# Softplus terms added on GpSimd and the head norm's factor kept in PSUM, in a two-layer block on one core

## The chip, the cores and the metric

One core of one Trainium2 chip runs the whole program. A core has five engines that take their instructions in order, each from a queue of its own, and wait for one another by semaphores: TensorE (PE: matmuls and weight loads), VectorE (DVE), ScalarE (ACT), GpSimd (POOL) and SyncE (SP, which here only issues DMAs). Data lies in SBUF; matmuls write PSUM, which VectorE and ScalarE can also read and write. The metric is the time of one execution on the device in microseconds, the median of the runs.

## The reference

2048 tokens (2 sequences of 1024) of width 512 pass four blocks, each followed by a layer norm of input plus output: linear attention with decay, a gated FFN whose hidden state passes a Walsh-Hadamard transform, a selective scan, and a second gated FFN. Two places matter here. The attention's output is gated, normed per head of 32 columns, and scaled:

```python
o = o * jax.nn.sigmoid(gate)
og = o.reshape(b, n, num_heads, hd)
og = og * jax.lax.rsqrt(jnp.mean(og * og, axis=-1, keepdims=True) + EPS)
return og.reshape(b, n, d) * w
```

and the scan's step width is a softplus, which multiplies the input:

```python
delta = jax.nn.softplus(dt + b_dt[None, None, :])
dA = jnp.exp(delta_t[:, :, None] * A[None])
dBu = (delta_t * u_t)[:, :, None] * B_t[:, None, :]
h = dA * h + dBu
```

All arithmetic is fp32.

## The kernel before

The tokens are cut into five groups, in this order: group 0 (256 tokens of sequence 0), group 1 (512 of sequence 1), group 2 (512 of sequence 0), group 3 (512 of sequence 1), group 4 (the last 256 of sequence 0). For each there are phases: V and A (values, then attention), F (first FFN), the scan, and f (second FFN). The second FFN of group 1 is split into a1 and b1, which with the first FFNs F0 and f0 (second FFN of group 0) serve as fillers: TensorE takes their work while an attention or a scan has none for it. The order of the end is V4, A4, b1, F4, f2, f3, f4.

Every operation is an `Op` with an engine, an estimated time, the buffers that it reads, writes, allocates and frees, and a priority. The class `Order` goes through all of them when the program is built: of the operations that could begin it takes the one that its own clock puts first, and so fixes each engine's order of instructions. An engine's instructions stay in that order on the chip, whatever the real times are. A changed estimate, engine or release of a buffer can thus change the order of everything behind it.

Four PSUM banks of 128x512 carry the tag "mm" and serve all matmul groups; the other four are two tiles "da" of two banks each, in which the scan's decays stand. An "mm" bank goes back to the planner when the operation that names it under `free` has run.

**The head norm** (in `block`, inside `attention`). The gated output stands in `oT` (SBUF; the trace shows it as xT). ScalarE squares it into `sg` (line 921), TensorE sums the squares of each head with a block matrix into an "mm" bank (line 931), ScalarE makes the factor in two steps (lines 939 and 940, `rstd`), both written into `sg`, and VectorE multiplies `oT` by the norm's weight and the factor in place (line 946, `scaled`). A group of 512 tokens has four such blocks with one multiply of 512 columns; a group of 256 has two blocks with two multiplies of 256 columns. That makes 16 blocks and 20 multiplies. The products L996 that follow (the output projection) read all blocks of `oT`.

**The softplus** (`Scan.softplus`). For each of four slices of 128 channels of a group, ScalarE takes the sum with the bias out of PSUM into `r` (tile pt, line 1297), then the absolute value, its exponential and logarithm in `a` (tile th, lines 1304 to 1306), and relu in `r` (line 1307). VectorE adds the two (line 1316). A DMA of SP's queue writes the result, delta, to DRAM; GpSimd multiplies it into `u` (line 1324); a second DMA of SP writes that. The scan's loads bring both back in another layout. Five groups of four slices make 20 adds.

**The scan** (per group, 64 units for 512 tokens or 32 for 256). GpSimd multiplies (line 1384, dbu), ScalarE exponentiates the decays into PSUM (line 1404), VectorE scans (line 1432) and multiplies by C (line 1445), and GpSimd sums the results into y by adds (lines 1475 and 1481) and, for every other unit, by a DMA of its own queue that accumulates. `ffn` has the line 1076, in which VectorE multiplies the two halves of a hidden tile: TensorE's second product (line 1099) waits for it. The transposes of the scan's result are line 1510, the add of the residual line 1525.

The estimates for one operation of n columns are, in us, 0.145 + 1.05e-3 n on VectorE (`dve`) and 0.15 + 2.25e-3 n on GpSimd (`pool`).

Of the kernel before, what the change touches and what calls it, by code (L numbers as in the profile page):

```python
# [10 lines left out]
AF = mybir.ActivationFunctionType  # L11
ALU = mybir.AluOpType
# [52 lines left out]
EXP, LOG, TANH, SILU = ("exp", "log"), ("log",), ("exp", "silu"), ("silu",)  # L65
# [144 lines left out]
def two_layers(  # L210
# [5 lines left out]
    nc = tc.nc  # L216
# [43 lines left out]
    def chunks(gi):  # L260
        return GROUPS[gi][2]

    def tokens(gi):
        return chunks(gi) * P
# [12 lines left out]
    def mm_us(n, cols):  # L277
        return n * max(cols * 4 / 2400 + 0.006, 0.28 if cols <= P else 0)

    def pe(us, fn, **kw):  # L280
        return Op("PE", us, fn, **kw)

    def dve(cols, fn, **kw):
        return Op("DVE", 0.145 + cols * 1.05e-3, fn, **kw)

    def act(cols, fn, **kw):
        return Op("ACT", 0.18 + cols * 0.81e-3, fn, **kw)

    def pool(cols, fn, **kw):
        return Op("POOL", 0.15 + cols * 2.25e-3, fn, **kw)  # L290

    def dma(nbytes, dst, src, eng="SP", **kw):
        of = {"SP": nc.sync, "ACT": nc.scalar, "POOL": nc.gpsimd}[eng]
        more = {k: kw.pop(k) for k in ("accum_op", "allow_slow_non_contiguous") if k in kw}
        us = 0.9 if eng == "POOL" else 0.06
        return Op(eng, us, lambda: of.dma_start(dst(), src(), **more), dma=nbytes, **kw)  # L296
# [99 lines left out]
    eps4 = cp.tile([P, 1], F32, name="eps4")  # L396
# [93 lines left out]
    def log_tables():  # L490

        if order.table != "log":
            nc.scalar.preload_act_table_set("natural_log_exp_and_others")  # L493
# [126 lines left out]
    def attention(gi, nxt, prio):  # L620
# [3 lines left out]
        n, T = chunks(gi), tokens(gi)  # L624
        S = CG // n
# [3 lines left out]
        oT = Columns(gi)  # L629
# [9 lines left out]
        parts = [Buf() for _ in range(VB)]  # L639

        def blocks(vb):
            return range(vb * S, (vb + 1) * S)
# [73 lines left out]
        def block(vb):  # L716

            kd, qd, own, sg = Buf(), Buf(), Buf(), Buf()
            bank = Buf()
# [159 lines left out]
            def outputs():  # L879
# [23 lines left out]
                r=[own, qd] + v2 + scs + ([] if first else [came]), a=[("mm", bank3)],  # L903
                free=[own, qd] + scs + (v2 if vb == VB - 1 else [])
# [7 lines left out]
            def gated():  # L912
                yield dve(
                    512, lambda: nc.vector.scalar_tensor_tensor(
                        o(), sg.t, 1.0, bank3.t, ALU.add, ALU.mult
                    ),
                    r=[sg, bank3] + ([oT.whole] if vb else []), w=[parts[vb]],
                    a=[] if vb else [("xT", oT.whole)], free=[bank3],
                )
                yield act(  # L920
                    512, lambda: nc.scalar.activation(
                        sg.t, o(), AF.Square, scale=1.0 / math.sqrt(HD)
                    ),
                    r=[parts[vb], oT.whole], w=[sg],
                )
                spawn(norm())

            def norm():
                bank = Buf()
                yield pe(  # L930
                    mm_us(1, 512), lambda: nc.tensor.matmul(
                        bank.t, blk, sg.t, start=True, stop=True
                    ),
                    r=[sg, consts_b], a=[("mm", bank)],
                )

                def rstd():
                    log_tables()
                    nc.scalar.activation(sg.t, bank.t, AF.Ln, bias=eps4)  # L939
                    nc.scalar.activation(sg.t, sg.t, AF.Exp, scale=-0.5)  # L940

                yield Op("ACT", 1.3, rstd, r=[bank], w=[sg], free=[bank], table=LOG)

                def scaled():
                    for s, eb in enumerate(blocks(vb)):
                        nc.vector.scalar_tensor_tensor(
                            oT.t[:, eb, :], oT.t[:, eb, :], nw_s[:, eb : eb + 1],
                            sg.t[:, s * T : (s + 1) * T], ALU.mult, ALU.mult,
                        )

                yield Op(
                    "DVE", 0.2 * S + 0.55, scaled, r=[sg, oT.whole], w=[parts[vb]], free=[sg]
                )
                normed[vb].written = parts[vb].written

# [249 lines left out]
    class Scan:  # L1205
# [83 lines left out]
        def softplus(self, k, bank, u):  # L1289

            T = self.T
            r = Buf()

            a = Buf()

            def shifted():
                nc.scalar.activation(
                    r.t[:, :T], bank.t[:, :T], AF.Identity, bias=bd_s[:, k : k + 1]
                )

            def logs():
                v = a.t[:, :T]
                log_tables()
                nc.scalar.activation(v, r.t[:, :T], AF.Abs)
                nc.scalar.activation(v, v, AF.Exp, scale=-1.0)
                nc.scalar.activation(v, v, AF.Ln, bias=one)
                nc.scalar.activation(r.t[:, :T], r.t[:, :T], AF.Relu)

            late = 1 if self.gi > 1 else 0
            yield act(T, shifted, r=[bank, scan_b], a=[("pt", r)], free=[bank])  # L1310
            yield Op(
                "ACT", 4 * (0.25 + T * 0.82e-3), logs, w=[r], a=[("th", a)], table=LOG,
                prio=late,
            )
            yield dve(
                T, lambda: nc.vector.tensor_add(r.t[:, :T], a.t[:, :T], r.t[:, :T]),
                r=[a], w=[r], free=[a], prio=late,
            )
            yield dma(
                KB256 * T // G, lambda: self.dd[0, :, k, :], lambda: r.t[:, :T], r=[r],  # L1320
                w=[self.parts_b[0][k]],
            )
            yield pool(
                T, lambda: nc.gpsimd.tensor_mul(u.t[:, k, :], r.t[:, :T], u.t[:, k, :]),
                r=[r, u.whole], w=[u_b := Buf()], free=[r],
            )
            yield dma(
                KB256 * T // G, lambda: self.dd[1, :, k, :], lambda: u.t[:, k, :],
                r=[u_b, u.whole], w=[self.parts_b[1][k]],
                free=[u.whole],  # L1330
            )
# [320 lines left out]
```

## Time and profile before

| what | value |
|---|---|
| runs | 1833.96, 1833.40, 1831.62 us |
| median | 1833.4 us |
| the profiled execution | 1834.95 us |
| its span, first to last instruction | 1833.2 us |
| mean granted TensorE clock | 0.989 |
| instructions of the program | 21,253 |
| HBM read and written | 253.12 and 22.54 MB |

| edited or touched | instructions | mean ns |
|---|---|---|
| head norm, logarithm (L939, ScalarE) 128x512 | 16 | 687 |
| head norm, exponential (L940, ScalarE) 128x512 | 16 | 630 |
| head norm, multiply (L946, VectorE) 128x256 | 8 | 482 |
| softplus multiply (L1324, GpSimd) 128x256 | 8 | 762 |
| scan (L1432, VectorE) 128x512 | 384 | 1226 to 1286 |
| product with C (L1445, VectorE) 128x1024 | 256 | 1223 |
| product du by B (L1384, GpSimd) 128x1024 | 256 | 2538 |

A busy share counts the time in which an engine executes; TensorE's matmuls are pipelined, so its share says little of how well it is used, but its gaps are gaps. An fp32 matmul appears as two records. "Idle before" a group is time in which its engine had nothing to execute just ahead of it, with what ended it. The granted clock is the share of its full speed that TensorE had.

### The profile page before, as it was taken

What the parts mean: (1) busy time and instruction counts of PE and PEld (TensorE: products, weight loads), DVE (VectorE), ACT (ScalarE), POOL (GpSimd) and SP (SyncE); (2) the same over time, 40 slices, a digit from 0 to 9 for tenths busy, and PEclk for the clock granted to TensorE, in tenths of its full rate; (3) what the DMA queues carried; (4) which work ended last, traced back from release to release, by engine and by line L of the source; (5) the groups of instructions that cost most, each with busy time, mean ns of one, the idle gap of its engine ahead of it and who ended that gap; (6) DMA issues with size and microseconds to landing.
All of it is one profiled execution on the core that took longest, in us unless ns stands there. A gap on an engine that the chain in (4) does not pass through costs nothing.

```text
span 1833.2 us, 21253 instructions
## 1 busy us (share of the span) xinstructions
PE 1769.9 (97%) x7064; PEld 1000.4 (55%) x7064; DVE 1308.5 (71%) x1557; ACT 1153.7 (63%) x1825; POOL 1069.8 (58%) x558
## 2 busy tenths in 40 slices
PE   7999999998999999999999999999999899999998
PEld 3556764443566644445675444577765344544574
DVE  6433115997699899926998999359998998998211
ACT  3634136688866776767766667676766757765321
POOL 0000004887477899824878888238899787786000
PEclk9999999999999999999999999999999999999999
DMA  9523435666657887736688676478988675766252
GB/s 265 180 68 106 149 128 166 179 179 173 230 138 217 245 212 207 192 113 197 171 255 232 167 207 181 143 243 236 282 234 222 187 199 167 199 169 166 75 174 85
DMA packets 227708, 336.32 MB, mean 183 GB/s; under 512 B 21264, under 2 KB 131216, under 8 KB 227600
## 3 DMA queue, kind: packets, MB, share of 16 engines
q1 hardware_dynamic: 209024, 271.53, 46.6%
q0 software_dynamic: 16272, 59.25, 17.1%
q10 hardware_dynamic: 2304, 4.20, 0.6%
q8 instruction: 56, 0.92, 0.2%
q14 instruction: 52, 0.43, 0.1%
HBM read 253.12 MB, written 22.54 MB: 150 GB/s over the span
## 4 chain that ended last, share of the span: by engine, by line
PE 67%; DVE 13%; ACT 8%; DMA 5%; issue 3%; POOL 3%; SPq 0%; DVEq 0%; ACTq 0%; POOLq 0%
PE mm L1045 35%; PE mm L1099 17%; DVE da L1432 6%; PE mm L653 4%; DMA y<-dbu 4%; PE mm L996 2%; PE mm L602 2%; POOL dbu L1384 2%; DVE dbu L1445 2%; ACT da L1404 2%; PE mm L840 1%; ACT L496 1%; ACT L1404 1%; PE mm L522 1%; ACT L493 1%
## 5 line engine op out<-in xcount | busy, mean ns | idle before, releaser
L1384 POOL TENSOR_TENSOR dbu<-du,B 128x1024 f32<-128x1024 f32 x256 | 646.9, 2538 | 141.3 <-DMA y<-dbu 107.8
L1045 PE MATMUL mm<-xT,w 128*128 128x512 f32 (+1 forms) x1912 | 669.1, 509 | 3.5 <-DVE h L1076 1.6
L1045 PEld LDWEIGHTS mm<-xT,w 128*128 128x128 f32 x1912 | 362.8, 190 | 308.4 <-issue 269.1
L1404 ACT ACTIVATE da<-delta,a_s 128x512 f32<-128x512 f32 (+1 forms) x640 | 384.3, 605 | 152.1 <-DVE dbu L1445 122.8
L1432 DVE TENSOR_TENSOR_SCAN da<-da,hlast,dbu 128x512 f32<-128x512 f32 (+1 forms) x384 | 425.7, 1109 | 34.0 <-ACT da L1404 20.4
L1099 PE MATMUL mm<-w,h 128*128 128x512 f32 x768 | 344.8, 605 | 9.7 <-DVE h L1076 7.4
L1481 POOL TENSOR_TENSOR y<-y,dbu 128x1024 f32<-128x1024 f32 x123 | 319.3, 2596 | 54.0 <-DVE dbu L1445 49.0
L1445 DVE TENSOR_TENSOR dbu<-da,C 128x1024 f32<-128x1024 f32 x256 | 313.1, 1223 | 14.9 <-ACT hlast L1457 7.9
L1432 DVE TENSOR_TENSOR_SCAN da<-da,dbu 128x256 f32<-128x256 f32 (+1 forms) x256 | 245.9, 960 | 20.9 <-ACT da L1404 14.9
L1099 PEld LDWEIGHTS mm<-w,h 128*128 128x128 f32 x768 | 147.6, 194 | 189.6 <-issue 170.4
L1045 PE MATMUL mm<-xf,w 128*128 128x256 f32 x1024 | 229.9, 383 | 2.3 <-ACT sg L939 1.4
L1045 PEld LDWEIGHTS mm<-xf,w 128*128 128x128 f32 x1024 | 194.7, 192 | 35.0 <-issue 4.6
L496 ACT ACT_TABLE_LOAD x140 | 179.6, 1283 | 6.9 <-PE mm L653 3.4
L496 ACT ACTIVATE h<-mm 128x512 f32<-128x512 f32 x144 | 85.7, 597 | 124.8 <-PE mm L1045 69.1
L1076 DVE TENSOR_TENSOR h<-h,mm 128x512 f32<-128x512 f32 x96 | 65.2, 679 | 101.8 <-PE mm L1045 94.7
L1404 ACT ACT_TABLE_LOAD x106 | 136.0, 1283 | 1.8
L653 PE MATMUL mm<-xT,w 128*128 128x512 f32 (+1 forms) x320 | 117.3, 514 | 7.6 <-DVE xn L1525 1.8
L1457 ACT COPY hlast<-da 128x2 f32<-128x2 f32 (+1 forms) x160 | 25.3, 158 | 156.1 <-DVE dbu L1445 140.1
L296 POOL DMA_DIRECT2D y<-dbu x113 | 107.8, 954 | 13.1 <-DVE dbu L1445 5.4
L743 POOL TENSOR_TENSOR qd<-h,q_dec 128x512 f32<-128x512 f32 x14 | 18.1, 1293 | 164.7 <-ACT h L496 104.5
L1099 PE MATMUL mm<-w,hf 128*128 128x512 f32 x256 | 112.5, 592 | 0.0
L1118 DVE TENSOR_TENSOR xn<-mm,xn 128x512 f32<-128x512 f32 x60 | 40.9, 682 | 93.8 <-PE mm L1099 93.8
(95 smaller groups left out, 1339.3 us busy)
## 6 DMA issues: line engine op xcount, KB each, us to landing
y<-dbu POOLq DMA_DIRECT2D x113, 512.0 KB, 6.1
w<-in_wgut_dram SPq DMA_DIRECT2D x192, 256.0 KB, 4.7
B<-rows SPq DMA_DIRECT2D x128, 256.0 KB, 4.7
C<-rows SPq DMA_DIRECT2D x128, 256.0 KB, 4.0
w<-in_wdnt_dram SPq DMA_DIRECT2D x96, 256.0 KB, 4.8
w<-in_w1t_dram SPq DMA_DIRECT2D x80, 256.0 KB, 4.4
w<-in_w3t_dram SPq DMA_DIRECT2D x80, 256.0 KB, 5.0
w<-w2h SPq DMA_DIRECT2D x80, 256.0 KB, 4.5
```

Source lines behind the costliest of these rows:

```text
L296: return Op(eng, us, lambda: of.dma_start(dst(), src(), **more), dma=nbytes, **kw)
L496: nc.scalar.activation(dst, src, AF.Silu)
L653: nc.tensor.matmul(bank.t[:, s * T : (s + 1) * T], w_qk[j][k].t[:, eb * P : (eb + 1) * P], xT.t[:, k, :], start=k == 0, stop=k == EB - 1,)
L1045: nc.tensor.matmul(bank.t[:, s * T + c0 * P : s * T + c1 * P], blocks[fb // 2][j][k // 2].t[:, k % 2 * 2 * P + k0 : k % 2 * 2 * P + k0 + P ...
L1076: 512, lambda: nc.vector.tensor_mul(t.t, t.t, pu.t), r=[pu], w=[t], free=[pu]
L1099: nc.tensor.matmul(accs[c].t, hT[f // S].t[:, s * T + c * P : s * T + (c + 1) * P], w_d[f].t, start=f == 0, stop=f == nt * S - 1,)
L1118: nc.vector.tensor_add(xb.t, bank.t, xb.t)
L1384: 1024, lambda: nc.gpsimd.tensor_mul(self.wide(self.db[i]), self.wide(du), self.row(self.bs, i)),
L1404: nc.scalar.activation(d[:, j, :], self.wide(delta)[:, j, :], AF.Exp, scale=a_s[:, k0 + j, n : n + 1],)
L1432: nc.vector.tensor_tensor_scan(d()[:, j, :], d()[:, j, :], self.wide(db)[:, j, :], init, ALU.mult, ALU.add,)
L1445: 1024, lambda: nc.vector.tensor_mul(self.wide(db), d(), self.row(self.cs, i)),
L1481: 1024, lambda: nc.gpsimd.tensor_add(y.t, y.t, db[i].t), r=o, w=[y],
```

## The change

The head norm's factor is no longer copied out of its PSUM bank: both steps of ScalarE write the bank that they read, VectorE's multiply reads the factor there, and the bank (with `sg`) is released after the multiply instead of after ScalarE's steps. The planner's estimates go from 1.3 to 1.4 us for ScalarE's pair and from 0.2 S + 0.55 to 0.15 S + 0.54 us for the multiply, S being 1 or 2 slices. The softplus add moves from VectorE to GpSimd with the same operands, priority and releases.

```diff
                 def rstd():
                     log_tables()
-                    nc.scalar.activation(sg.t, bank.t, AF.Ln, bias=eps4)
-                    nc.scalar.activation(sg.t, sg.t, AF.Exp, scale=-0.5)
-
-                yield Op("ACT", 1.3, rstd, r=[bank], w=[sg], free=[bank], table=LOG)
+                    nc.scalar.activation(bank.t, bank.t, AF.Ln, bias=eps4)
+                    nc.scalar.activation(bank.t, bank.t, AF.Exp, scale=-0.5)
+
+                yield Op("ACT", 1.4, rstd, r=[bank], w=[bank], table=LOG)
 
                 def scaled():
                     for s, eb in enumerate(blocks(vb)):
                         nc.vector.scalar_tensor_tensor(
                             oT.t[:, eb, :], oT.t[:, eb, :], nw_s[:, eb : eb + 1],
-                            sg.t[:, s * T : (s + 1) * T], ALU.mult, ALU.mult,
+                            bank.t[:, s * T : (s + 1) * T], ALU.mult, ALU.mult,
                         )
 
                 yield Op(
-                    "DVE", 0.2 * S + 0.55, scaled, r=[sg, oT.whole], w=[parts[vb]], free=[sg]
+                    "DVE", 0.15 * S + 0.54, scaled, r=[bank, sg, oT.whole], w=[parts[vb]],
+                    free=[bank, sg],
                 )
...
-            yield dve(
-                T, lambda: nc.vector.tensor_add(r.t[:, :T], a.t[:, :T], r.t[:, :T]),
+            yield pool(
+                T, lambda: nc.gpsimd.tensor_add(r.t[:, :T], a.t[:, :T], r.t[:, :T]),
                 r=[a], w=[r], free=[a], prio=late,
             )
```

## The prediction

> **What bounds the kernel now.** I read the busy shares first, then the stretches of 50 us, then TensorE's own waits, and last the instructions of the two edited places. The first row of the page, with two of the stretches (window, then busy us and count for PE, PEld, DVE, ACT, POOL, then granted clock, DMA share, GB/s):
>
> ```profile
> PE 1769.9 (97%) x7064; PEld 1000.4 (55%) x7064; DVE 1308.5 (71%) x1557; ACT 1153.7 (63%) x1825; POOL 1069.8 (58%) x558
> ...
> 1450.00:1500.00 50.00, 45.47 (x100) 19.67 (x99) 47.85 (x44) 28.60 (x38) 40.02 (x22) 0.93 0.73 196
> ...
> 1550.00:1600.00 50.00, 50.00 (x142) 26.64 (x141) 46.51 (x67) 37.23 (x70) 38.77 (x20) 1.00 0.65 178
> ```
>
> TensorE is busy for 1769.9 of 1833.2 us and, from 1550 us to its last matmul at 1827 us, without a break. So an edit off TensorE can only move the 63.3 us in which it is idle, and the stretches at half clock that follow some of its gaps. In the stretch from 1450 us the mean granted clock is 0.93; the clock's records give 0.5 for 6.8 us from 1460.5, which loses 3.4 us. Next, the edited groups and their nearest relatives (count, then busy us and mean ns, then idle before):
>
> ```profile
> L1316 DVE TENSOR_TENSOR pt<-th,pt 128x256 f32<-128x256 f32 x8 | 13.0, 1621 | 10.8 <-ACT pt L1307 10.4 <-DMA w<-w2h 0.4
> L1316 DVE TENSOR_TENSOR pt<-th,pt 128x512 f32<-128x512 f32 x12 | 8.3, 693 | 34.0 <-ACT pt L1307 31.0 <-DMA dd<-pt 2.0 <-issue 0.8
> L946 DVE SCALAR_TENSOR_TENSOR xT<-xT,nw,sg 128x512 f32<-128x512 f32 x12 | 15.2, 1270 | 2.5 <-ACT sg L940 2.4
> L914 DVE SCALAR_TENSOR_TENSOR xT<-sg,mm 128x512 f32<-128x512 f32 x16 | 10.9, 682 | 13.9 <-PE mm L895 13.0 <-DMA dm<-dmh 0.9
> L1324 POOL TENSOR_TENSOR xT<-pt,xT 128x512 f32<-128x512 f32 x12 | 15.2, 1268 | 51.4 <-DVE pt L1316 49.2 <-PE mm L653 2.2
> ```
>
> The 256-wide adds average 1621 ns and the twice as wide ones 693. All four 256-wide adds of group 0 took 0.42 to 0.43 us with GpSimd idle; the four of group 4 took 3.48, 0.90, 5.29 and 1.60 us, each beside a running GpSimd multiply or add. L946 shows the same: 0.74 us alone, up to 2.16 us beside GpSimd, while L914, the same form with one operand in PSUM, never passes 0.69 us. So in this trace a VectorE instruction with both operands in SBUF stands still while GpSimd streams. Last, the time line where the worst of them stands (start, us, engine, line):
>
> ```profile
> 1439.49 5.29 DVE L1316 TENSOR_TENSOR pt<-th,pt 128x256 f32<-128x256 f32 x1
> 1441.56 2.94 POOL L1384 TENSOR_TENSOR dbu<-du,B 128x1024 f32<-128x1024 f32 x1
> 1442.88 3.70 PE L1045 MATMUL mm<-xT,w 128*128 128x512 f32 x8 [1.40 <-ACT h L496]
> ...
> 1447.16 0.68 DVE L1076 TENSOR_TENSOR h<-h,mm 128x512 f32<-128x512 f32 x1
> ...
> 1447.89 3.70 PE L1045 MATMUL mm<-xT,w 128*128 128x512 f32 x8 [1.31 <-DVE h L1076]
> ...
> 1457.42 1.60 DVE L1316 TENSOR_TENSOR pt<-th,pt 128x256 f32<-128x256 f32 x1
> ...
> 1462.13 18.29 PE L1099 MATMUL mm<-w,h 128*128 128x512 f32 x36 [4.53 <-DVE h L1076]
> ```
>
> The FFN product L1076 queues behind the stalled add in VectorE's order, and TensorE waits for it: 1.31 us, then 4.53 us, then the half clock.
>
> **Part A: the adds go to GpSimd.** Off VectorE: 8.3 + 13.0 = 21.3 us, of which group 4's four are 3.48 + 0.90 + 5.29 + 1.60 = 11.3 us in a stretch where VectorE is 88 to 96% busy. The other sixteen stand where VectorE idles before them (L1316's idle time is 44.8 us), so taking them away is worth nothing there. Of TensorE's three waits I count the two that end at L1076, 1.31 + 4.53, and the half clock after the second, 3.4: 9.2 us. The second wait follows a late silu, L496 at 1460.16; ScalarE had idled 2.03 us and 2.45 us before it for VectorE (scan and product), more than half of the wait, so earlier VectorE work reaches it too. The wait of 1.40 us for L496 stays. GpSimd pays for four 256-wide adds, by L1324's four undisturbed times of 0.72 us: 2.9 us; its own instructions that stood beside the locked adds took 3.22, 3.19 and 2.94 instead of 2.64, 2.35 and 2.64, which gives 1.7 us back. Net 1.2 us later on GpSimd, charged in full. A: -9.2 + 1.2 = **-8.0 us**. Bounds: 0 (all of it returns at the next wait) to -10.6 (the 1.40 goes as well and GpSimd's charge is hidden).
>
> GpSimd executes in order, so the add now waits there for ScalarE's L1307, with the products L1384, the sums L1481 and the accumulating DMAs of its queue behind it, and behind those the scans of VectorE. VectorE waited 2.46 us for L1307 at the first of the four; a GpSimd queue that waited as long at each would lose 9.8 us. That is a rival below; in the sum 0, since GpSimd's next instruction for the same term, L1324, waited only 0.44 us twice. SP's queue gets the same two DMAs per term.
>
> The Trainium skill, "GPSIMD Engine Reference", section 4.1, speaks against this: elementwise work belongs to VectorE, GpSimd being about half as fast on two inputs. By it alone the move costs GpSimd 4 more adds at twice 0.43 us and gains nothing. The mean of the four locked adds, 2816 ns on VectorE against 0.72 us on GpSimd, turns that round here, and I go by it.
>
> **Part B: the head norm's multiply, L946, reads the bank.** Priced by L914: in group 2 the four took 0.97 + 1.68 + 1.37 + 1.85 = 5.87 us and become 4 x 0.682 = 2.73; in group 3, 6.39 us becomes 2.73. That is 6.8 us of VectorE. But TensorE waits only once for L946, 1.3 us ahead of L996, in group 0 where it is not locked. VectorE's other late results around these places, L914 0.7 and L810 0.5 us, bound a gain at about 3 us in the two attentions together. I take **0**. ScalarE's pair L939 and L940 (687 + 630 ns) now writes PSUM and reads it twice. Reading PSUM: 587 ns (L773) against 630 (L1304) from SBUF; writing it: 689 (L1404) against 722 (L1306), both with a pointer operand. So between no change and 16 x 0.11 = 1.7 us less of ScalarE: 0.
>
> **Part C: the bank is held longer.** It was free when L939 ended; now only when L946 has. From L939's end to L946's start plus 0.682 us is 1.38, 1.38, 1.98, 2.74 us in group 2 and 1.97, 2.58, 1.84, 2.06 us in group 3: 15.9 us. Two matmul groups waited for exactly this release, L1045 at 513.96 (1.38 us) and L653 at 853.27 (1.21 us); they would start 1.38 and 1.97 us later, 3.4 us, unless the planner, which knows the later release, puts other work ahead. Half: **+1.7 us**; bounds 0 and 15.9.
>
> The skill's page "ScalarE: Activation LUTs", section "Step-by-step: what each stage is for", calls PSUM the destination with less latency, useful only if TensorE does not need most of PSUM. The rows agree on the first (33 ns); the second is the case here, since four banks are "mm" and the other four "da"; by the page the edit gains those 33 ns and warns of Part C.
>
> **Part D: scans start later.** The last add of each 512-wide group takes about 1.27 us (L1324) instead of 0.69: 0.58 us later to the write of delta and the start of the scan. While a scan runs TensorE has FFN work to cover this; only at the end of scan 3, near 1531 us, did it wait for the last sums (1.55 us, then 1.52 for the bank that L1525 frees). One end of four: **+0.6 us**; bounds 0 and 4 x 0.58 = 2.3.
>
> **Sum:** -8.0 + 0 + 1.7 + 0.6 = -5.7 us. The profiled execution took 1834.95 us (span 1833.2, 1.75 around it), 1.55 above the median of the runs: 1829.25 there, **1827.7** as a median.
>
> **The rivals.** *Given back at the end of scan 3.* TensorE reaches the transposes L1510 at 1531 us, in order, and waits for GpSimd's last sum. If GpSimd sets that scan's pace, TensorE arrives 9.2 us earlier and waits 9.2 us more: about 1833.4. For it: GpSimd waits 18.3 us for its accumulating DMAs between 1350 and 1540. Against: in the same stretch ScalarE waits 41.6 us for VectorE's product alone, and VectorE for GpSimd only 4.6. *The bank* (slower): all 15.9 us of the held bank reach TensorE, with two half-clock windows of 3.4 us (1.7 each): 1833.4 - 8.0 + 15.9 + 3.4 + 0.6 = 1845.3. It decides from 11.1 us of the 15.9, where it outweighs 8.0 - 0.6 by 3.7. For it: two of the eight were waited for at once, and attention fills the four banks. Against: the other six were not. *GpSimd's queue blocked:* 9.8 us for L1307 and 2.9 for the adds push scan 3's end, 12.7 us: 1846.1. *It does not do what it says:* the multiply stays locked though one operand is in PSUM; L914 says no, and it would give 1833 to 1836.
>
> **How the numbers follow.** A change of 0.2%, 3.7 us, is about what a measurement of this kernel tells from none. Likeliest, 0.45: the forecast, own range 1819 to 1829.7. Given back, with no effect at all: 0.23, within 0.2%. Bank 0.20, queue 0.10, both slower. No unlocking 0.02. The planner orders everything after the first edit anew by its costs, so waits of 1 to 2 us move both ways; that and the bounds (-10.6 - 3 - 4.8 for the waits and half clock near 1531, against the two slow rivals) make the range 1816 to 1845. Faster 0.46, same 0.23, slower 0.31.
>
> **What would show it.** A: no L1316 on VectorE, twenty adds on GpSimd at 0.72 and 1.27 us, the waits for L1076 of 1400 to 1465 gone and no half clock there. B: L946's successor at 0.68 us at most. C: waits of TensorE that end at L946. The prediction is wrong if TensorE's idle time does not fall, or if GpSimd's wait for L1307 in group 4 passes 8 us.

## The result and the profile after

| | before | after |
|---|---|---|
| median of 13 runs each, us | 1831.69 | 1835.81 |
| lowest and highest, us | 1829.45, 1834.72 | 1834.18, 1837.68 |
| profiled execution and its span, us | 1834.95, 1833.2 | 1835.34, 1833.6 |

After over before is 1.0022 (95% interval 1.0013 to 1.0031): about 4 us slower, where 5.7 us faster was forecast. The two profiled spans differ by only 0.4 us, because the profiled execution of before lies 3.3 us above the median of its runs and that of after 0.5 us below its own. So the traces are compared stage by stage, and 1 or 2 us between two traces are not taken as a finding.

The page of after, span and busy time of each engine:

```profile
span 1833.6 us, 21255 instructions
...
PE 1769.4 (97%) x7064; PEld 1000.8 (55%) x7064; DVE 1281.9 (70%) x1537; ACT 1163.8 (63%) x1833; POOL 1088.0 (59%) x578
```

VectorE has lost 20 instructions and 26.6 us, GpSimd has gained 20 and 18.2 us, and TensorE is busy for the same 1769 us. ScalarE has 8 instructions and 10.1 us more, though the change gives it none: those are eight more table loads of 1.28 us (322 instead of 314), the first sign that the order has changed. The edited groups (count, then busy us and mean ns, then idle before):

```profile
L1318 POOL TENSOR_TENSOR pt<-th,pt 128x512 f32<-128x512 f32 x12 | 15.2, 1266 | 45.0 <-ACT pt L1309 45.0
L1318 POOL TENSOR_TENSOR pt<-th,pt 128x256 f32<-128x256 f32 x8 | 8.1, 1010 | 20.1 <-ACT pt L1309 20.1
L947 DVE SCALAR_TENSOR_TENSOR xT<-xT,nw,mm 128x512 f32<-128x512 f32 x12 | 8.9, 738 | 2.2 <-ACT mm L941 2.1
L940 ACT ACTIVATE mm<-mm,eps 128x512 f32<-128x512 f32 x16 | 10.6, 662 | 4.2 <-PE mm L931 4.0
L941 ACT ACTIVATE mm<-mm 128x512 f32<-128x512 f32 x16 | 9.3, 582 | 0.5
```

(Code behind the edit has moved down: the adds are L1318, the head norm's multiply L947, the FFN product L1078.) Both edits do locally what they say: the 512-wide multiply averages 738 ns instead of 1270, and no add is left on VectorE.

The 1010 ns of the 256-wide adds needs care, because GpSimd's records overlap: one starts before the record ahead of it has ended. The second add of group 4 with its neighbours:

```profile
1439.55 2.93 POOL L1483 TENSOR_TENSOR y<-y,dbu 128x1024 f32<-128x1024 f32 x1
1441.86 1.30 POOL L1318 TENSOR_TENSOR pt<-th,pt 128x256 f32<-128x256 f32 x1
1442.54 2.92 POOL L1386 TENSOR_TENSOR dbu<-du,B 128x1024 f32<-128x1024 f32 x1
```

The sum ahead ends at 1442.48 and the add at 1443.16, so the add takes 0.68 us from end to end, whatever its record says. The records of the four adds of group 4 read 1.86, 1.30, 1.02 and 1.01 us; from end to end each takes 0.68.

The stretches around group 4's softplus and the end of scan 3, where the forecast gain lay (busy us of TensorE, its weight loads, VectorE, ScalarE, GpSimd, then the granted clock, DMA share and GB/s):

```profile
1400.00:1450.00 50.00, 49.71 (x140) 25.55 (x139) 41.26 (x40) 43.85 (x62) 49.49 (x30) 1.00 0.76 202
1450.00:1500.00 50.00, 49.50 (x116) 21.77 (x115) 46.23 (x42) 29.95 (x41) 42.77 (x25) 1.00 0.85 219
1500.00:1550.00 50.00, 44.80 (x123) 21.61 (x122) 44.54 (x58) 40.60 (x63) 38.44 (x19) 0.97 0.65 190
sum 150.00, PE 144.01 PEld 68.92 DVE 132.03 ACT 114.40 POOL 130.70; mean PE 48.00 PEld 22.97 DVE 44.01 ACT 38.13 POOL 43.57
```

In the second stretch TensorE goes from 45.47 to 49.50 us and the clock from 0.93 to 1.00. Add TensorE's idle time and what the clock takes (one less the clock, by 50 us for each row, so to about half a microsecond): before lost 150 - 139.32 = 10.7 idle and 0.07 x 50 + 0.03 x 50 = 5.0 to the clock, 15.7 us in all; after loses 6.0 + 1.5 = **7.5**. The stretch gained 8.2 us, 4.7 of them idle time. The clock's part is less certain: after the same gap of 4.5 us the half clock lasts 6.8 us in before and 3.4 us in the head norm only (below), so 1 or 2 us of it can be the one execution. What TensorE waits for there, between 1400 and 1540 us (total, times, longest):

```profile
PE mm L1512 <- POOL y L1483: 4.3, 1, 4.3
PE mm L1101 <- DVE h L1078: 0.5, 1, 0.5
PE mm L1047 <- DVE h L1078: 0.3, 1, 0.3
```

Of the waits for the FFN product that of 1.31 us is gone and that of 4.53 us has come down to 0.5 (the 0.3 stands in before too, at 1406 us); the wait at the end of scan 3 went from 1.55 to 4.3 us.

So the question is not why the gain failed to come, but what took it. When stages end on TensorE, by the time lines, in us:

| end on TensorE of | before | after | adds only (below) | adds on GpSimd, order of before (below) |
|---|---|---|---|---|
| softplus matmuls, group 2 | 817.6 | 822.8 | 820.7 | 816.8 |
| output projection, group 3 | 911.1 | 918.3 | 916.5 | 908.3 |
| softplus matmuls, group 4 | 1406.1 | 1414.4 | 1413.4 | 1404.5 |
| transposes of scan 3 | 1536.8 | 1537.0 | 1537.7 | 1532.6 |
| last matmul | 1826.8 | 1827.2 | 1827.7 | 1822.1 |

After comes to group 4's softplus 8.3 us late, and the 8 us that it gains there only bring it level. Of the 8.3 us, 1.5 are there from the start (group 0's output projection ends at 99.4 us instead of 97.9); most of the rest is lost between the end of the attention of group 2 (562 us) and that of group 3, while scan 1 still runs until 794 us. These are stages that the prediction did not look at for Part A because VectorE idles before their adds. Since the profiled execution of before lies above its median, the last column is the better measure: its kernel measures like before (0.9996), and its execution lies 0.6 us below its own median. Against it after comes to group 4 9.9 us late and gains 6.3 us in the stretch (13.8 us lost there, below, against 7.5), which leaves 3.6 us, close to the 4 measured.

### The profile page after: what moved, and what is told of

Same layout as the page of the kernel before. It is cut to its first block, busy times and chain, and to the rows that moved or that the text cites. A ratio compares the mean times of both kernels' runs of the same rounds, so it can differ in the third digit from the quotient of the medians.

```text
span 1833.6 us, 21255 instructions
## 1 busy us (share of the span) xinstructions
PE 1769.4 (97%) x7064; PEld 1000.8 (55%) x7064; DVE 1281.9 (70%) x1537; ACT 1163.8 (63%) x1833; POOL 1088.0 (59%) x578
## 4 chain that ended last, share of the span: by engine, by line
PE 54%; DVE 18%; ACT 10%; DMA 6%; POOL 6%; issue 6%; SPq 0%; DVEq 0%; ACTq 0%
PE mm L1047 27%; PE mm L1101 14%; DVE da L1434 10%; DMA y<-dbu 4%; PE mm L653 4%; POOL dbu L1386 3%; DVE dbu L1447 3%; ACT da L1406 2%; POOL y L1483 2%; ACT L496 2%; ACT L1406 2%; PE mm L998 1%; PE mm L602 1%; PE mm L840 1%; PE mm L1182 1%
## 5 line engine op out<-in xcount | busy, mean ns | idle before, releaser
L1483 POOL TENSOR_TENSOR y<-y,dbu 128x1024 f32<-128x1024 f32 x123 | 323.9, 2633 | 49.2 <-DVE dbu L1447 48.8
L1101 PE MATMUL mm<-w,h 128*128 128x512 f32 x768 | 340.0, 598 | 8.0 <-DVE h L1078 3.1
L1078 DVE TENSOR_TENSOR h<-h,mm 128x512 f32<-128x512 f32 x96 | 65.2, 679 | 111.4 <-PE mm L1047 97.1
```

The costliest lines, as they stand in the source:

```text
L1078: 512, lambda: nc.vector.tensor_mul(t.t, t.t, pu.t), r=[pu], w=[t], free=[pu]
L1101: nc.tensor.matmul(accs[c].t, hT[f // S].t[:, s * T + c * P : s * T + (c + 1) * P], w_d[f].t, start=f == 0, stop=f == nt * S - 1,)
L1483: 1024, lambda: nc.gpsimd.tensor_add(y.t, y.t, db[i].t), r=o, w=[y],
```

## The experiments

Theories. **O** (order): the booking of an add on GpSimd makes the planner order the middle groups anew, and that order costs more than the moved work gains. **W** (work): the adds on GpSimd themselves, longer and in GpSimd's queue, delay the scans. **B** (bank): holding the bank delays TensorE. **T** (tables): the additional table loads are the cost. Each ratio is to the kernel before on the same chip, with its 95% interval.

### Which half of the change, and its booking apart from its work

The planner takes an operation's engine and time from `dve` or `pool`; the instruction that is emitted is named separately. So the engine can move at the old order, and the order can change at the old engine.

**Adds only** (the change without the head norm's part).

```diff
-            yield dve(
-                T, lambda: nc.vector.tensor_add(r.t[:, :T], a.t[:, :T], r.t[:, :T]),
+            yield pool(
+                T, lambda: nc.gpsimd.tensor_add(r.t[:, :T], a.t[:, :T], r.t[:, :T]),
```

> The adds move to GpSimd, in the planner too; the head norm is as before. Theory of the order: the sum of the two runs above, so between 4 us faster and 4 us slower than before. Rival (the held bank is what costs): 5 to 9 us faster, as forecast for this part. Rival (GpSimd's queue): 3 us or more slower.

Measured: 1.0026 (1.0012 to 1.0040).

**Head norm only** (with the estimates and releases of the change).

```diff
-                    nc.scalar.activation(sg.t, bank.t, AF.Ln, bias=eps4)
-                    nc.scalar.activation(sg.t, sg.t, AF.Exp, scale=-0.5)
+                    nc.scalar.activation(bank.t, bank.t, AF.Ln, bias=eps4)
+                    nc.scalar.activation(bank.t, bank.t, AF.Exp, scale=-0.5)
...
-                            sg.t[:, s * T : (s + 1) * T], ALU.mult, ALU.mult,
+                            bank.t[:, s * T : (s + 1) * T], ALU.mult, ALU.mult,
```

> The head norm's factor stays in its PSUM bank until VectorE's multiply; the adds stay on VectorE. Theory of the order: anything from 3 us faster to 6 us slower, as this order falls. Rival (the held bank): 5 to 12 us slower, with waits of TensorE in attention that end at the multiply.

Measured: 0.9985 (0.9975 to 0.9995). The loss is the adds'; the head norm's part helps.

**Adds on GpSimd at the order of before.** TensorE, ScalarE and SyncE keep exactly the instruction order of before.

```diff
             yield dve(
-                T, lambda: nc.vector.tensor_add(r.t[:, :T], a.t[:, :T], r.t[:, :T]),
+                T, lambda: nc.gpsimd.tensor_add(r.t[:, :T], a.t[:, :T], r.t[:, :T]),
```

> The softplus adds run on GpSimd, but the planner still books them as VectorE's, so that every other instruction keeps the order of before. Theory (the new order costs what the unlocking gains): at the old order the unlocking shows alone, 4 to 9 us faster than before, with TensorE's waits of 1.3 and 4.5 us near 1447 and 1462 us gone. Rival (GpSimd's queue, blocked by the adds, is what costs): 2 us or more slower. Rival (the adds give nothing, all returns at the end of scan 3): within 2 us.

Measured: 0.9996 (0.9984 to 1.0007). The 4 to 9 us that were expected did not come. The wait of 1.3 us went and that of 4.5 us fell only to 3.0, and at the end of scan 3 TensorE waits 5.5 us for GpSimd's last sum instead of 1.6.

**The new order at the old engine.**

```diff
-            yield dve(
+            yield pool(
                 T, lambda: nc.vector.tensor_add(r.t[:, :T], a.t[:, :T], r.t[:, :T]),
```

> The adds stay on VectorE, but the planner books them as GpSimd's with GpSimd's estimate, so that the order is the one of the adds alone and the engine is the old one. Theory of the order: slower than before by 2 to 8 us. Rival (GpSimd's queue): the same as before within 2 us, since no add is on GpSimd.

Measured: 1.0053 (1.0038 to 1.0067), some 10 us, a little more than expected. The four cases together:

| | order of before | new order |
|---|---|---|
| adds on VectorE | 1 | 1.0053 |
| adds on GpSimd | 0.9996 | 1.0026 |

From left to right is the order alone: +0.53% and +0.30% (10 and 5.5 us). Downward is the engine alone: nothing that can be told at the old order, -0.27% (5 us) at the new one. O stands, W falls: the moved work costs nothing that can be told. The order's cost shows at the start of the last transposes of scan 1 and the matmuls behind them. TensorE's time line (start, us, engine, line) of the adds at the order of before:

```profile
790.71 2.04 PE L1510 MATMUL mm<-cst,y 128*128 128x128 f32 x16
...
806.14 3.60 PE L1246 MATMUL mm<-xT,wbc 128*128 128x512 f32 x8
```

and of the new order with the adds still on VectorE:

```profile
788.36 7.13 PE L1099 MATMUL mm<-w,h 128*128 128x512 f32 x16 [1.33 <-ACT h L496]
...
799.20 2.04 PE L1510 MATMUL mm<-cst,y 128*128 128x128 f32 x16
...
809.14 3.27 PE L1246 MATMUL mm<-xT,wbc 128*128 128x512 f32 x7 [2.93 <-ACT xT L529]
```

With no add on GpSimd, the transposes still come 8.5 us later than in the first fence (7.7 us later than in before, 791.51), behind sixteen L1099 matmuls in one lot instead of between two lots of eight. The next stage, L1246, then waits 2.93 us for ScalarE's copy L529 of transposes that now stand directly before it. Scan 1's last sum on GpSimd ended at 783.9 us in before, 783.1 at the order of before with moved adds, 792.3 and 793.1 in the two kernels with the new order, 794.0 in after.

What VectorE's adds do at the new order, and GpSimd's (shortest, median and longest in ns):

```profile
L1316 DVE TENSOR_TENSOR pt<-th,pt x20: 407/691/3844, 272.3 to 1469.7; 128x512 f32<-128x512 f32 x12, 128x256 f32<-128x256 f32 x8
```

```profile
L1316 POOL TENSOR_TENSOR pt<-th,pt x20: 722/1264/1925, 272.5 to 1468.3; 128x512 f32<-128x512 f32 x12, 128x256 f32<-128x256 f32 x8
```

The first fence is the new order with the adds on VectorE, the second the adds only: the worst add goes from 3.84 us on VectorE to a record of 1.93 us on GpSimd, 0.68 from end to end. TensorE loses 15.4 us from 1400 to 1550 us in the first and 10.5 in the second (table below): this is where the engine earns its 5 us.

### The table loads

Scan 1 begins late in the new order: its first sum on GpSimd starts at 512.9 us in after, 511.2 and 511.4 in the two kernels above with the new order, 501.7 with the moved adds at the order of before (before: 499.3). In the new order ScalarE loads two more tables between the first and the second slice's logarithms of that group; the slices share the single buffer th, which the add frees. A second th buffer lets the slices follow one another:

```diff
-    for name, n in (("dm", 2), ("th", 1), ("kd", 1), ("qd", 1), ("sg", 2), ("sc", 4), ("g1", 1)):
+    for name, n in (("dm", 2), ("th", 2), ("kd", 1), ("qd", 1), ("sg", 2), ("sc", 4), ("g1", 1)):
```

With the adds on GpSimd:

> The adds on GpSimd, booked as GpSimd's, the head norm as before, and two buffers th instead of one. Theory (the single th, released later by the slower engine, makes the planner let other work with other ScalarE tables in between the slices of a softplus): the table loads fall from 322 back to 314 or fewer, scan 1 starts some 5 us earlier than in the run with the adds alone, and the time is 4 us or more below that run's (ratio to before 0.995 to 1.001). Rival (the new order is bad for another reason): 1.002 to 1.005 again.

Measured: 1.0023 (1.0010 to 1.0037), with 314 loads again. And the kernel before with that line alone:

> The kernel before with two buffers th: the control for the run above. Theory: VectorE's add frees th early enough, so 0.997 to 1.002. Rival (a second th is a gain of its own, whoever adds): under 0.997.

Measured: 1.0061 (1.0046 to 1.0077), a plain miss. The loads went and the time stayed, which speaks against T but does not exclude it, since the second buffer makes a new order with a cost of its own. The count of loads at least does not follow the time: this slowest kernel has 316, and so has the fastest of the next section. With the second buffer and the adds on GpSimd, scan 1's first product on GpSimd even started on time (483.1 us; before 482.8), and yet its last sum ended at 794.7 us, so there the time is lost in the course of the scan and not ahead of it. The miss is worth more than the test: one buffer more, with nothing added but two table loads and nothing moved to another engine, costs 11 us. The planner chose another order: TensorE's differs from 479 us on.

### Which groups

The planner is told of GpSimd, and the adds are put there, for chosen groups alone; the rest is as before.

```diff
-            yield dve(
-                T, lambda: nc.vector.tensor_add(r.t[:, :T], a.t[:, :T], r.t[:, :T]),
+            yield (pool if self.gi == 4 else dve)(
+                T, lambda: (nc.gpsimd if self.gi == 4 else nc.vector).tensor_add(
+                    r.t[:, :T], a.t[:, :T], r.t[:, :T]
+                ),
```

Group 4 alone, whose four adds were the ones that stood still:

> Only the four adds of the last group, the ones that stood locked beside GpSimd, go to GpSimd; groups 0 to 3 keep VectorE; the head norm is as before. Theory: the order up to some 1400 us is the one of before, so the loss near 470 and 800 us is gone and the gain of the unlocking stays: ratio 0.995 to 0.999. Rival (the gain of unlocking always returns at the end of scan 3): 0.999 to 1.001. Rival (GpSimd's booking is bad in the last group too): over 1.002.

Measured: **0.9962** (0.9947 to 0.9976), 7 us. Its stretches:

```profile
1400.00:1450.00 50.00, 49.72 (x119) 21.96 (x118) 40.31 (x36) 44.88 (x62) 45.66 (x28) 1.00 0.81 218
1450.00:1500.00 50.00, 49.44 (x116) 21.77 (x115) 47.00 (x43) 27.89 (x37) 44.31 (x26) 1.00 0.82 210
1500.00:1550.00 50.00, 43.73 (x124) 22.01 (x124) 41.74 (x58) 39.04 (x65) 38.05 (x18) 0.93 0.51 158
```

The first two rows are as good as in after. The third gives some back: 43.73 busy where before had 46.93, and a clock of 0.93 for 0.97. Its time line shows why:

```profile
1519.61 0.44 PE L1512 MATMUL mm<-cst,y 128*128 128x128 f32 x2
1525.64 2.40 PE L1512 MATMUL mm<-cst,y 128*128 128x128 f32 x10 [5.60 <-POOL y L1483]
```

TensorE comes to these transposes at 1519.6 us instead of 1530.9 and waits 5.60 us for GpSimd's last sum instead of 1.55. TensorE's own order is that of before up to 1577 us; what the planner moved before that is work of ScalarE, VectorE and GpSimd.

Groups 1 and 4 (condition `self.gi in (1, 4)`):

> The adds of groups 1 and 4 on GpSimd, those of groups 0, 2 and 3 on VectorE; the head norm as before. Theory (booking group 1's adds on GpSimd reorders the second attention and starts scan 1 late): against the run with the last group alone (0.9962) it loses 3 to 6 us, ratio 0.998 to 1.001, and the transposes of scan 1's result come near 800 us instead of 791. Rival (the loss is in group 2 or 3): 0.995 to 0.997.

Measured: 0.9986 (0.9975 to 0.9998). All but group 1 (`self.gi != 1`):

> All adds on GpSimd but those of group 1; the head norm as before. Theory: the loss at scan 1 is gone (transposes near 791 us), what remains is the loss in the third attention, which group 2's adds reorder: 3 to 5 us above the run with the last group alone, ratio 0.998 to 1.000. Rival (all the loss is group 1's): 0.995 to 0.997.

Measured: 1.0002 (0.9991 to 1.0013), just above what was expected. Where scan 1's transposes stand in the two, first groups 1 and 4, then all but group 1:

```profile
795.98 2.04 PE L1512 MATMUL mm<-cst,y 128*128 128x128 f32 x16
```

```profile
791.10 2.04 PE L1512 MATMUL mm<-cst,y 128*128 128x128 f32 x16
```

Moving and booking group 1's adds on GpSimd makes scan 1 late (795.98 against 790.86 with group 4 alone) and costs 0.24%, some 4 us (the two intervals just touch); with the move alone, at the order of before, the transposes stood at 790.71. Leaving group 1 out brings the transposes back to time, but the output projection of group 3 then ends at 914.5 us, where it ended at 908.5 with group 4 alone: 6 us that the earlier groups' booking still costs, in the attention of group 3. So the loss has two places, and no single group makes it.

### The bank

The head norm's order, estimates and late release as in the change, but with the factor copied to SBUF as before:

```diff
-                yield Op("ACT", 1.3, rstd, r=[bank], w=[sg], free=[bank], table=LOG)
+                yield Op("ACT", 1.4, rstd, r=[bank], w=[sg], table=LOG)
...
-                    "DVE", 0.2 * S + 0.55, scaled, r=[sg, oT.whole], w=[parts[vb]], free=[sg]
+                    "DVE", 0.15 * S + 0.54, scaled, r=[bank, sg, oT.whole], w=[parts[vb]],
+                    free=[bank, sg],
```

> The order of the head norm alone (0.9985), the bank held until the multiply as in the change, but the factor copied to SBUF as before, so that the multiply reads two SBUF operands beside GpSimd again; adds on VectorE. Theory: the multiplies of groups 2 and 3 take 1.0 to 2.2 us again, the time is 0 to 4 us above the norm alone, ratio 0.998 to 1.001. Rival (the held bank costs, and unlocking the multiply hides it): over 1.002.

Measured: 0.9999 (0.9986 to 1.0012). The trace shows that this run does not test B as it was meant to. The planner takes the bank as held until the multiply, and TensorE's order is that of the head norm only, but nothing reads the bank after the logarithm, and on the chip the next matmuls are let go by the logarithm. TensorE in group 2 and in group 3, here:

```profile
514.94 2.50 PE L1047 MATMUL mm<-xf,w 128*128 128x256 f32 x5 [1.38 <-ACT sg L940]
...
851.43 2.84 PE L653 MATMUL mm<-xT,w 128*128 128x512 f32 x6 [1.21 <-ACT sg L940]
```

and in the head norm only, where the bank is read by the multiply and really held:

```profile
513.32 3.72 PE L1047 MATMUL mm<-xf,w 128*128 128x256 f32 x16 [0.78 <-DVE sc L858]
...
851.58 2.84 PE L653 MATMUL mm<-xT,w 128*128 128x512 f32 x6 [0.19 <-DVE sc L858]
```

The same two places at the same point of the order. Held, the bank is not the one that the next matmuls get: they get one that VectorE's L858 frees, and wait 0.78 and 0.19 us instead of 1.38 and 1.21. So B falls by the head norm only (0.9985 with the bank held), and with the sign turned round: holding the bank took 1.6 us of wait away at these two places. The multiply in the run of this section, and then in the head norm only:

```profile
L947 DVE SCALAR_TENSOR_TENSOR xT<-xT,nw,sg x20: 477/744/2042, 72.5 to 1219.3; 128x512 f32<-128x512 f32 x12, 128x256 f32<-128x256 f32 x8
```

```profile
L947 DVE SCALAR_TENSOR_TENSOR xT<-xT,nw,mm x20: 472/728/747, 72.2 to 1218.7; 128x512 f32<-128x512 f32 x12, 128x256 f32<-128x256 f32 x8
```

The longest is 2042 ns with the factor in SBUF and 747 with it in PSUM, in the same order: that is the operand. Operand and bank together make 0.9985 against 0.9999, some 2.6 us, though the two intervals overlap; what each has of it was not measured apart.

### Parts put together

The whole change, but with all adds booked as VectorE's (diffs above joined):

> The changed kernel, but with the adds on GpSimd booked as VectorE's. Theory: the norm's part (0.9985 alone) and the adds at the old order (0.9996 alone) add up: 0.996 to 0.999. Rival (the two parts get in each other's way): over 1.000.

Measured: 0.9986 (0.9976 to 0.9996), against 1.0022 for the change: once more 0.36% for the booking alone, with every add on GpSimd in both. The head norm's part with group 4's adds alone:

> The head norm of the change, and of the adds only the last group's on GpSimd: the parts that gained. Theory (the parts add up where neither reorders the early groups badly): 0.9985 times 0.9962, that is 0.994 to 0.997. Rival (each order is a new draw): anywhere from 0.996 to 1.003.

Measured: 0.9964 (0.9948 to 0.9980). It came out like group 4 alone. 0.9985 x 0.9962 is 0.9947, just outside this interval, but with the intervals of the two factors it cannot be told whether the parts add.

All twenty adds on GpSimd, but only group 4's booked there; first without the head norm's part, then with it, which is the changed kernel with nothing but the booking of sixteen adds undone (the diff shows the second, against after):

```diff
-            yield pool(
+            yield (pool if self.gi == 4 else dve)(
                 T, lambda: nc.gpsimd.tensor_add(r.t[:, :T], a.t[:, :T], r.t[:, :T]),
```

> All 20 adds run on GpSimd; the planner books those of groups 0 to 3 as VectorE's and those of group 4 as GpSimd's; the head norm as before. Theory (the early adds cost only through the order that their booking makes): like the last group alone, 0.995 to 0.998. Rival (running them on GpSimd, at 1.27 us instead of 0.69 ahead of each scan, costs by itself): 0.999 to 1.002.

> The changed kernel whole, every instruction on the engine that the change gives it, with only the booking of the adds of groups 0 to 3 left as VectorE's. Theory: the loss of the change was the booking, so 0.994 to 0.998, as the norm with the last group's adds (0.9964). Rival (the change's work itself is slower): 1.001 or more.

Measured: 0.9975 (0.9963 to 0.9986) and **0.9970** (0.9957 to 0.9983). Telling the planner of group 4's four adds seems to be a gain in itself: 0.9975 where none was told of gave 0.9996, with intervals that just overlap. The last one runs the work of the changed kernel on the same engines (with 316 table loads instead of 322), at 0.9970 instead of 1.0022. What remains of the waits between 1400 and 1540 us in it:

```profile
PE mm L1512 <- POOL y L1483: 5.5, 1, 5.5
PE mm L1101 <- DVE h L1078: 0.7, 1, 0.7
```

and where scan 1's transposes stand:

```profile
791.73 2.04 PE L1512 MATMUL mm<-cst,y 128*128 128x128 f32 x16
```

Group 4 is served as in after, scan 1 is on time: the change's loss is the order of the groups before the last. The two fastest kernels, group 4's adds alone with and without the head norm's part, cannot be told apart, and both beat before and after.

TensorE's losses from 1400 to 1550 us, worked out as above (idle, clock), show what group 4 needs:

| | idle | clock | lost, us |
|---|---|---|---|
| before | 10.7 | 5.0 | 15.7 |
| new order, adds on VectorE | 10.4 | 5.0 | 15.4 |
| order of before, adds on GpSimd | 10.3 | 3.5 | 13.8 |
| adds only (both new) | 7.0 | 3.5 | 10.5 |
| group 4's adds alone (both new) | 7.1 | 3.5 | 10.6 |
| after | 6.0 | 1.5 | 7.5 |

Neither the engine (1.9 us) nor the order (0.3 us) is worth much alone there; together they give 5.2 us. In idle time alone, without the uncertain clock, it is 0.4, 0.3 and 3.7 us.

## Why the prediction was wrong, step by step

**The step that failed** is the sentence "The planner orders everything after the first edit anew by its costs, so waits of 1 to 2 us move both ways". It was used to widen the range, and the sum had no term for it. The runs put that term at +10 us (1.0053), nearly all of it in groups 1 to 3: the new order with the adds still on VectorE ends group 4's softplus matmuls at 1413.1 us, the order of before with the adds on GpSimd at 1404.5. The sixteen adds that the prediction valued at nothing there cost nothing that can be told by being moved; they cost by being booked. With the engine's 5 us back (-0.27%) and the head norm's 2.7 (0.9985) the parts come to about +2; the whole measured +4, with an interval of 1.6 us to either side. For Part A the prediction looked only at the groups where the moved work itself mattered. One of its own signs of being wrong came true: TensorE's idle time did not fall (63.3 us of the span before, 64.2 after).

**Part A, -8.0.** The mechanism holds and so, by accident, does the size: the stretch gained 8.2 us, the wait for L1076 at 1447 us is gone, that at 1462 is down to 0.5 us, and no half clock follows. But the prediction gave all of it to the engine. At the order of before the engine alone saved 1.9 us of that stretch, 1.5 of them clock, and the wait of 4.53 us shrank only to 2.98:

```profile
1447.52 6.17 PE L1099 MATMUL mm<-w,h 128*128 128x512 f32 x14
1456.67 5.85 PE L1099 MATMUL mm<-w,h 128*128 128x512 f32 x13 [2.98 <-DVE h L1076]
```

(TensorE, adds on GpSimd, order of before.) The prediction's own remark that ScalarE had idled for VectorE more than once before this wait was right; that taking four adds away would mend it all was not. The rest needed the planner to know of the move and reorder group 4. The price of 0.72 us for a 256-wide add on GpSimd held: 0.72 in group 0, and 0.68 from end to end in group 4, 2.7 us for the four instead of 2.9. But the 1.7 us that GpSimd was to get back were misread from its overlapping records: from end to end the three instructions with records of 3.22, 3.19 and 2.94 us took 2.39, 2.30 and 2.39, and all the products and sums of after lie between 2.29 and 2.41. Without that term Part A would have been -6.3. The Trainium skill, "GPSIMD Engine Reference", section 4.1, which gives elementwise work to VectorE, would have had the move lose by itself. On the speed the trace agrees (1266 ns for a 512-wide add on GpSimd, 693 on VectorE), but no run shows a loss from the move itself: 0.9996 at the old order and -0.27% at the new one.

**The wait behind the add on GpSimd,** priced at 0, was right. From 1395 to 1475 us GpSimd in after waits for nothing but DMAs:

```profile
POOL dbu L1386 <- DMA y<-dbu: 2.8, 2, 2.5
POOL y L296 <- DMA y<-dbu: 0.5, 1, 0.5
```

The rival of the blocked queue falls.

**Part B, 0 on the path.** The mechanism is shown: with one operand in PSUM the multiply no longer stands still (749 ns at most in after). Priced at 682 ns, it takes 738; twelve 512-wide ones went from 15.2 to 8.9 us. The whole edit gave 2.7 us alone (0.9985), near the bound of 3 that the prediction named and then put at nothing; up to 1.6 of it may be the bank's. The order that came with the edit gave nothing: with it and the factor in SBUF the ratio was 0.9999. ScalarE's pair fell from 687 + 630 to 662 + 582 ns, 73 ns per block, within the bounds given. The first step, of which only the destination changed, fell by 25 ns. This agrees with the lower latency that the Trainium skill's page "ScalarE: Activation LUTs", section "Step-by-step: what each stage is for", states for PSUM as a destination; its condition, that TensorE must not need most of PSUM, did not bite here (0.9985 with the bank held).

**Part C, +1.7,** had the wrong sign. The step that failed is that the two matmul groups that waited for L939 "would start 1.38 and 1.97 us later": the sum took it that they would wait for the same bank for longer. They were given another one, and waited 0.6 and 1.0 us less. No matmul of after waits for the multiply but L998, the output projection, 1.2 us, as L996 did in before (1.3). The rival of the bank falls.

**Part D, +0.6,** cannot be separated. GpSimd's last sum of scan 3 let TensorE go at 1533.65 us in after and at 1532.83 in before, 0.8 us later, but the scan's start had been shifted by the order too.

**Given back at the end of scan 3** was true in part. With group 4's adds alone 5.60 us were waited for instead of 1.55, and the clock's loss there grew from 1.5 to 3.5 us; still 7 us came out at the end.

**Not settled:** what in the new order makes scan 1 late. The test of the table loads speaks against them but brought an order of its own. Nor is it settled whether the gains of the head norm and of group 4 add.

## What to carry to other kernels

Where a program orders its instructions by booked costs, move an instruction's engine twice: once with the old booking, which shows what the work is worth, and once with the booking alone, which shows what the order is worth. Move only the instructions that the trace shows standing still: four of twenty adds, moved and booked, gave 0.38%, all twenty lost 0.26%. A stalled VectorE instruction with two SBUF operands can also be cured in place, by leaving one operand in PSUM.

## What had not been expected of the hardware

The stall has an exact end. In before, each of the four adds of group 4 ended 0.28 or 0.29 us after the record of a GpSimd product or sum, however long it had stood. The longest, 5.29 us, started while one product ran, did not get in when that ended at 1441.28 us, and ended 0.29 us after the next product, which itself had started 2 us later than the add. The seven 512-wide multiplies that stalled all ended 0.55 us after such an instruction. GpSimd pays little for it. Beside the standing adds its products and sums kept to 2.30 to 2.39 us from end to end, although their records reach 3.22. Six of them in all of before took 2.68 to 2.79 us, each next to a 512-wide multiply of the head norm; in after, where the factor stands in PSUM, none takes more than 2.41.

And the time that a stalled operation costs depends on what stands behind it. In the order of before the longest add on VectorE takes 5.29 us, and with the adds on GpSimd the end does not move (0.9996); in the new order the longest takes 3.84 us, and the end comes 5 us sooner.
